# Relative attention and routed FFN on one core: the four weight tiles of a step turned in one stretch, the relative values in the bank of the value products

## The chip, the cores and the metric

The kernel is one program on one core of a Trainium2 chip. The metric is the device time of one execution in microseconds (us); lower is better. Timed runs of the same kernel are reported by their median. A profiled execution gives a trace with the start and duration of every instruction on every engine: PE is the matrix engine (TensorE; PEld are its weight loads), DVE the vector engine, ACT the scalar engine, POOL the general engine, SP the queue that issues most DMAs.

## The reference

The input is `x` of shape (16, 512, 128): 16 batches of 512 positions with 128 features. Everything is float32.

```python
q, k, v = proj(Wq, bq), proj(Wk, bk), proj(Wv, bv)      # 16 heads of 8 features, x normalized first
idx = clip(r[None, :] - r[:, None], -M, M) + M          # M = 128: relative place, cut at +-128
rpk, rpv = rel_k[idx], rel_v[idx]                        # (S, S, 8)
scores = (einsum('bhqd,bhkd->bhqk', q, k) + einsum('bhqd,qkd->bhqk', q, rpk)) / sqrt(8)
w = softmax(scores)
out = einsum('bhqk,bhkd->bhqd', w, v) + einsum('bhqk,qkd->bhqd', w, rpv)
x = x + layernorm(out @ Wo.T + bo)
# then: layernorm, top-1 routing to 16 experts, gated expert FFN and a shared FFN, layernorm, added to x
```

The second product of `out` needs, for each query, the weights of the keys that lie within 128 places of it times the relative values `rel_v`. Keys farther off all take the first or the last row of `rel_v`; the kernel adds those rows to `v` instead.

## The kernel before

**Two stages.** The attention stage computes all 16 batches and writes routed rows to DRAM; the FFN stage then reads blocks of 128 rows of one expert each. The change is in the attention stage alone.

**Steps.** The attention stage is one loop over steps `i`, 16 to a batch. `at(i)` gives batch `b`, unit `c` (one of 4) and `n` (one of 4); below, *step k* is the place `i % 16` in a batch, so `n` is `k % 4`. A step treats 32 queries and all 16 heads as four tiles of 128 x 512 scores, one for each head group `g` in the order `ORDER = (0, 2, 1, 3)`. They are called the first, second, third and fourth tile. All engines' instructions of this stage are kept in program order (the class `InOrder`, which is line 47 of every record), so the order of the lines of the loop is the order in each engine's queue.

**What a step does before the change.** In the order of the program:

- `scores` (PE): the content products (`ps<-kT,qb`, 32-row tiles of the array) and then the relative ones (`ps<-relk,qr`, 64-row tiles) into four PSUM banks of the pool `ps_s`. The relative ones go over a window of keys, 160 to 288 wide, which depends on the step; it is 288 wide in half of the steps.
- `turn` of the first and second tile of the step before (PE): four 128 x 128 transposes each (`pt<-ident,w`) into a bank of the pool `ps_t`, which has two.
- `peak` (DVE) and `exps` (ACT) of the first and second tile: the row maximum `nmax` and the exponentials `w` with their row sums. A score bank is free again when its `exps` is done.
- the copies of the two turned tiles out of PSUM to `wT`: the first by DVE, the second by ACT.
- `peak` and `exps` of the third and fourth tile.
- `attend` of the step five back (PE): the products of `wT` with the values (`pa<-wT,v`, 32-column tiles), into the first 128 columns of a bank of the pool `ps_o`, which has one; where `n == 1` also `join_places` (`pa<-oz,msum`) into the next 128 columns. Its `leave` runs at once: DVE copies out the join (`oj`), multiplies `pa` by the reciprocal sums and the head mask `Rh` (`od`) and adds the heads up (`oT`).
- `attend_near` of the same step (PE): the products with the relative values (`pz<-wT,relv`, 24 of them). They gather over the four steps of a unit in a bank of their own, `ps_z`; after the fourth DVE multiplies the whole bank by `Rz` in two instructions of 256 columns into `oz`.
- `turn` of the third tile and its copy by DVE.
- a spare job where there is one (`prt` in steps with `n == 0`, the output product `py` with `n == 1`, work for the next batch in steps 6, 7, 14 and 15), all in the one bank of `ps_o`.
- `turn` of the fourth tile and its copy by ACT. It needs the bank of the second tile.
- statistics and the routing of the batch before (`route`), a slice per step with `n > 0`: mostly small DVE work, and in a few steps a product in the bank of `ps_o` (`pr` in step 1, `ptf` in step 11, `pl` in step 13).

PE reads the transposed tiles four steps later, so the turn itself is not urgent. Four score banks, two of `ps_t`, one of `ps_o` and one of `ps_z` make up the eight banks of PSUM.

Of the kernel before, what the change touches and what calls it, by code (L numbers as in the profile page):

```python
# [9 lines left out]
F32 = mybir.dt.float32  # L10
# [4 lines left out]
PSUM = bass.MemoryType.PSUM  # L15
DRAM = bass.MemoryType.DRAM

P = 128
# [6 lines left out]
NKT = S // P  # L25
HG = 4
HH = H // HG
TQ = 8
# [22 lines left out]
def relative_attention_then_moe(  # L51
# [42 lines left out]
    with ExitStack() as actx:  # L94
# [3 lines left out]
        up = actx.enter_context(tc.tile_pool(name="attn_unit", bufs=2))  # L98
        sp = actx.enter_context(tc.tile_pool(name="attn_small", bufs=4))
        ps_s = actx.enter_context(tc.tile_pool(name="ps_s", bufs=4, space=PSUM))  # L100
        ps_t = actx.enter_context(tc.tile_pool(name="ps_t", bufs=2, space=PSUM))
        ps_o = actx.enter_context(tc.tile_pool(name="ps_o", bufs=1, space=PSUM))
        ps_z = actx.enter_context(tc.tile_pool(name="ps_z", bufs=1, space=PSUM))
        pe, act, dve, sp_q, pool = (InOrder(tc, e) for e in (nc.tensor, nc.scalar, nc.vector, nc.sync, nc.gpsimd))


# [323 lines left out]
        def join_places(pj, b, c):  # L430

            oz = batch.pop((b, c, "oz"))
            for h in range(HH):
                pe.matmul(
                    pj[h * 32 : (h + 1) * 32, :], msum.rearrange("p g d -> p (g d)"),
                    oz[:, h].rearrange("p t f q -> p (t f q)"), start=True, stop=True,
                )
            oj = up.tile([P, P], F32, tag="oj", name=f"oj{b}_{c}")
            batch[b, c, "oj"] = oj
            return lambda: dve.tensor_copy(oj, pj)  # L440

        def attend(b, c, n, done=None):


            wT = wts[b, c][0]
            v = batch[b]["v"]
            Rh = batch[b, c, "R"][0]
            if n == 0:
                batch[b, c, "oT"] = up.tile([P, NKT * 4, TQ], F32, tag="oT", name=f"oT{b}_{c}")
            oT = batch[b, c, "oT"]  # L450
            both = bank([P, 2, P], f"pa{b}_{c}_{n}")
            pa = both[:, 0]
            for kt in range(NKT):
                vn = 1 if kt <= n - 2 else 2 if kt >= n + 2 else 0
                for g in range(HG):
                    r = slice(g * 32, (g + 1) * 32)
                    pe.matmul(
                        pa[r, :], v[:, vn, kt, r], wT[:, n, g, (kt - n) % NKT, :],
                        start=(kt == 0), stop=(kt == NKT - 1),
                    )  # L460
            t = slice(n * 4, n * 4 + 4)
            summed = join_places(both[:, 1], *done) if done is not None else lambda: None

            def leave():
                summed()
                od = up.tile([P, 4, HH, TQ], F32, tag="od", name=f"od{b}_{c}_{n}")
                dve.tensor_mul(od, pa.rearrange("p (t h q) -> p t h q", h=HH, q=TQ), Rh[:, t])
                dve.tensor_reduce(oT[:, t], od.rearrange("p t h q -> p t q h"), AX.X, ALU.add)

            return leave  # L470

        def attend_near(b, c, n):


            wT = wts[b, c][0]
            if n == 0:
                batch[b, c, "pz"] = ps_z.tile([P, NKT, 8, HH, 4], F32, tag="z", name=f"pz{b}_{c}")
            pz = batch[b, c, "pz"]
            for u in (2 * n, 2 * n + 1):
                for k, n0, n1 in ((0, 0, 4), (3, 1, 4), (1, 0, 3)):  # L480
                    a = (P if k == 1 else -P if k == 3 else 0) - c * 32 - u * 4 + 252
                    for g in range(HG):
                        r = slice(g * 32, (g + 1) * 32)
                        pe.matmul(
                            pz[r, n0:n1, u],
                            relv[:, a : a + 4, :].rearrange("p t d -> p (t d)"),
                            wT[:, n0:n1, g, k, :].rearrange("p n (t h f q) -> p n t h f q", t=4, h=HH, f=2)[
                                :, :, u // 2, :, u % 2, :
                            ],
                            start=(k == 0), stop=(k == 1),  # L490
                        )
            if n < NKT - 1:
                return lambda: None
            wts.pop((b, c))
            Rz = batch.pop((b, c, "R"))[1]
            oz = up.tile([P, HH, NKT * 4, 2, 4], F32, tag="oz", name=f"oz{b}_{c}")
            batch[b, c, "oz"] = oz

            def leave():
                for f in range(2):  # L500
                    dve.tensor_mul(
                        oz[:, :, :, f, :].rearrange("p h t q -> p t h q"),
                        pz.rearrange("p n (t f) h q -> p (n t) f h q", f=2)[:, :, f],
                        Rz[:, :, :, f, :],
                    )

            return leave

# [217 lines left out]
        for i in range(total + 24):  # L726
            b, c, n = at(i)
            k = i % 16
            last = i - 1 if 0 <= i - 1 < total else None
            old = i - 5 if 0 <= i - 5 < total else None  # L730
            live = i < total
            done = at(i - 9)[:2] if n == 1 and 0 <= i - 9 < total else None
            nxt = b + 1 if b + 1 < B else None

            spare = None
            if 0 < b < B and k == 6:
                routes[b - 1, 0] = route(b - 1)

            if i == total + 1:
                routes[b - 1, 0] = route(b - 1, 0, NC - 1)  # L740
            if i == total + 5:
                routes[b - 1, 1] = route(b - 1, NC - 1, NC)
            if n == 0 and 0 <= i - 4 < total:
                sums(*at(i - 4)[:2])
                spare = lambda: sums_turn(*at(i - 4)[:2])
            if n == 1 and i >= 9 and i - 9 < total:
                spare = lambda: output(*at(i - 9)[:2])
            if 10 <= i < 30:
                clear_rows((i - 10) * NBLK // 20, (i - 9) * NBLK // 20)
            if nxt is not None:  # L750
                if k == 0 and b + 2 < B:
                    load_x(b + 2)
                if k in (6, 7, 14, 15):
                    f = {6: x_turn, 7: queries, 14: keys, 15: values}[k]
                    spare = lambda: f(nxt)

            if live:
                scores(b, c, n)
            if last is not None:
                T = {g: turn(*at(last), g) for g in ORDER[:2]}  # L760
            if live:
                peak(b, c, n, ORDER[0])
                peak(b, c, n, ORDER[1])
                exps(b, c, n, ORDER[0])
                exps(b, c, n, ORDER[1])
            if last is not None:
                dve.tensor_copy(*T[ORDER[0]])
                act.copy(*T[ORDER[1]])
            if live:
                peak(b, c, n, ORDER[2])  # L770
                peak(b, c, n, ORDER[3])
                exps(b, c, n, ORDER[2])
                exps(b, c, n, ORDER[3])
            if old is None and done is not None:
                join_places(bank([P, P], f"pj{b}"), *done)()
            if old is not None:
                attend(*at(old), done=done)()
                scale = attend_near(*at(old))
            if last is not None:
                dve.tensor_copy(*turn(*at(last), ORDER[2]))  # L780
            if old is not None:
                scale()
            if spare is not None:
                leave = spare()
            if last is not None:
                act.copy(*turn(*at(last), ORDER[3]))
            if spare is not None:
                leave()
            if nxt is not None and k in (0, 2):
                x_stats(nxt, k)  # L790
                x_stats(nxt, k + 1)
                if k == 2:
                    x_norm(nxt)

            for r in sorted(routes):


                turns = (n > 0) if nxt is not None else {7: 2, 9: 0, 12: 0, 13: 2, 15: 2}.get(k, 1) if live else 1
                for _ in range(turns):
                    bank_user = next(routes[r], StopIteration)  # L800
                    if bank_user is StopIteration:
                        del routes[r]
                        break
                    elif bank_user is not None:
                        bank_user()()
            if n == 1 and i + 3 < total:
                expand(*at(i + 3)[:2])
# [163 lines left out]
```

## Time and profile before

| | |
|---|---|
| median of 3 runs | 1973.37 us (1972.97 to 1974.53) |
| profiled execution | 1977.44 us, its span 1975.7 us |
| mean granted TensorE clock | 0.989 |
| PE busy | 1905.7 us (96%), 41070 matmuls |
| PEld busy | 1518.6 us (77%) |
| DVE busy | 1539.5 us (78%), 3922 instructions |
| ACT busy | 1154.3 us (58%) |
| POOL busy | 901.3 us (46%) |
| score matmuls (`ps`), first and last start | 23.0 and 1689.8 us |

Busy shares are averages over both stages. Matmuls overlap, so the time that a group of them holds PE is read from the starts of one group and the next, not from durations.

### The profile page before, as it was taken

The numbers are of one execution on the slowest core, as the hardware profiler recorded it, in microseconds if no ns is written. First come the engines' busy times: TensorE is split into PE (matmuls) and PEld (weight loads), VectorE is DVE, ScalarE is ACT, GpSimd is POOL, SyncE is SP. The second block draws the span as 40 slices with busy tenths as digits, with TensorE's granted clock in tenths as the row PEclk, the third lists the DMA queues.
The fourth block names the chain that finished last, engine by engine and source line by source line (L and its number), as shares of the span: only waits on it lengthen the run. The fifth ranks groups of instructions, "written<-read, shape, count | busy, mean of one in ns | idle before, by whom it ended". The sixth has DMA issues, their size and how long they took to land.

```text
span 1975.7 us, 92844 instructions
## 1 busy us (share of the span) xinstructions
PE 1905.7 (96%) x41070; PEld 1518.6 (77%) x41070; DVE 1539.5 (78%) x3922; ACT 1154.3 (58%) x2929; POOL 901.3 (46%) x1007
## 2 busy tenths in 40 slices
PE   6999999999999999999999999999999999689997
PEld 3777777777777777777777777777777777589997
DVE  4677787888787878787878888787878787757776
ACT  3666566666656666666666666666666666234432
POOL 4234454444444453535453544444444534246666
PEclk9999999999999999999999999999999999889999
DMA  2312000000000000000000000000000000066553
GB/s 75 69 30 42 14 23 5 14 14 6 22 5 24 5 23 3 25 3 25 3 25 3 25 3 16 12 12 16 5 18 5 18 7 5 13 176 176 173 165 95
DMA packets 88342, 68.94 MB, mean 35 GB/s; under 512 B 26439, under 2 KB 74340, under 8 KB 87808
## 3 DMA queue, kind: packets, MB, share of 16 engines
q1 hardware_dynamic: 81248, 53.60, 10.5%
q0 software_dynamic: 4384, 8.57, 1.2%
q8 instruction: 323, 5.29, 1.1%
q10 hardware_dynamic: 2304, 0.80, 0.2%
q14 instruction: 83, 0.68, 0.1%
HBM read 44.79 MB, written 18.75 MB: 32 GB/s over the span
## 4 chain that ended last, share of the span: by engine, by line
PE 80%; POOL 8%; DVE 6%; issue 5%; ACT 1%; DMA 1%; POOLq 0%; ACTq 0%; DVEq 0%; SPq 0%
PE ps L47 27%; PE pt L47 24%; PE pa L47 13%; PE pz L47 7%; POOL out_dram L912 4%; DVE nmax L47 3%; POOL lf_rs L80 2%; PE prt L47 2%; PE py L47 2%; POOL f L910 2%; PE pq L47 1%; PE pl L47 1%; PE pv L47 1%; PE pk L47 1%; DVE wT L47 1%
## 5 line engine op out<-in xcount | busy, mean ns | idle before, releaser
L47 ACT ACTIVATE w<-ps,nmax 128x512 f32<-128x512 f32 x1024 | 699.3, 693 | 497.7 <-DVE nmax L47 497.7
L47 DVE TENSOR_REDUCE nmax<-ps 128x1 f32<-128x512 f32 x1024 | 656.2, 683 | 288.3 <-PE ps L47 288.3
L47 PE MATMUL pt<-ident,w 128*128 128x128 f32 x4096 | 590.8, 280 | 3.1 <-DVE wT L47 2.7
L47 PEld LDWEIGHTS pt<-ident,w 128*128 128x128 f32 x4096 | 446.5, 141 | 139.0 <-issue 98.7
L47 ACT COPY wT<-pt 128x512 f32<-128x512 f32 x512 | 299.9, 586 | 129.0 <-PE pt L47 129.0
L47 DVE COPY wT<-pt 128x512 f32<-128x512 f32 x512 | 349.3, 682 | 1.6 <-PE pt L47 1.5
L47 PE MATMUL ps<-kT,qb 32*128 32x288 f32 (+10 forms) x4864 | 327.1, 375 | 5.4 <-POOL qb L47 3.8
L47 PE MATMUL pa<-wT,v 128*32 128x128 f32 x8192 | 276.7, 276 | 2.0 <-ACT R L47 1.2
L47 PE MATMUL ps<-relk,qr 64*32 64x288 f32 (+4 forms) x8192 | 275.2, 377 | 0.0
L47 PEld LDWEIGHTS ps<-kT,qb 32*128 32x128 f32 x4864 | 208.9, 186 | 62.9 <-issue 35.3
L47 PEld LDWEIGHTS pa<-wT,v 128*32 128x32 f32 x8192 | 208.0, 109 | 44.3 <-issue 41.6
L47 POOL TENSOR_TENSOR Rh<-R,mh 128x512 f32<-128x512 f32 x64 | 66.5, 1039 | 357.7 <-ACT R L47 351.2
L47 ACT ACTIVATION_READ_ACCUMULATOR w<-ps,nmax 128x1 f32 x1024 | 212.5, 208 | 0.0
L47 PEld LDWEIGHTS ps<-relk,qr 64*32 64x32 f32 x8192 | 124.4, 106 | 112.8 <-issue 82.8
L47 PE MATMUL pz<-wT,relv 128*32 128x48 f32 (+1 forms) x12288 | 192.1, 210 | 1.3 <-issue 1.3
L47 PEld LDWEIGHTS pz<-wT,relv 128*32 128x32 f32 x12288 | 184.1, 110 | 1.9 <-issue 1.9
L47 POOL TENSOR_TENSOR qr<-qz,mq 128x1024 f32<-128x1024 f32 x64 | 137.7, 2152 | 0.0
L47 POOL TENSOR_SCALAR kT<-kT,kend 128x512 f32<-128x512 f32 x32 | 49.8, 1562 | 145.0 <-ACT sg L47 128.3
L47 DVE TENSOR_REDUCE oT<-od 128x32 f32<-128x128 f32 x256 | 97.6, 381 | 8.9
L875 ACT ACTIVATE x2b<-x2b,xc 128x128 f32<-128x128 f32 x73 | 29.0, 401 | 125.2 <-DVE lf_ve L78 114.0
L47 POOL COPY rb<-rt 128x512 f32<-128x512 f32 x64 | 39.0, 609 | 116.6 <-DVE rt L47 104.7
L47 POOL DMA_INDIRECT rows<-pay,at_i x64 | 68.0, 1062 | 51.9 <-DVE shift L47 41.4
(157 smaller groups left out, 2241.8 us busy)
## 6 DMA issues: line engine op xcount, KB each, us to landing
gu<-_L_ffn_gate_up_proj_dram SPq DMA_DIRECT2D x73, 256.0 KB
dn<-in_L_ffn_down_proj_dram SPq DMA_DIRECT2D x73, 128.0 KB
rows<-zero SPq DMA_DIRECT2D x19, 266.0 KB
xc<-rows SPq DMA_DIRECT2D x8, 532.0 KB
x_sb<-in_L_attn_x_dram SPq DMA_DIRECT2D x64, 64.0 KB
qd<-qp SPq DMA_DIRECT2D x16, 256.0 KB
qz<-qd SPq DMA_DIRECT2D x248, 16.0 KB
relv<-vext SPq DMA_DIRECT2D x1, 1536.0 KB
```

Of the source, the lines that this page charges most:

```text
L47: return lambda *a, **k: self.tc.keep_in_program_order(op(*a, **k))
L80: root.tensor_tensor(rs, ve, mhalf[:, 0:n], ALU.pow)
L875: nc.scalar.mul(x2[:, 1, :], x2[:, 0, :], x[:, D + 2 : D + 3])
L910: nc.gpsimd.tensor_add(f, f, x[:, 0:D])
L912: own_rows("out", nc.gpsimd.indirect_dma_start(out_rows, bass.IndirectOffsetOnAxis(ap=to, axis=0), f, None, bounds_check=B * S - 1, oob_is ...
```

## The change

The pool `ps_t` gets a third bank and `ps_z` goes; PSUM stays at eight banks. A step is now `scores`, all four `peak` and `exps`, then on PE the values, the join and the near products, and then all four turns in one stretch, and after them the spare job. DVE copies the first tile after its four `peak`, ACT the second after its four `exps`; the fourth tile is turned into the bank of the first. The near products no longer gather over a unit: they go into columns 256 to 383 of the bank of the values, in the order (n, h, f, q), in runs of 4 columns instead of 16, and each step multiplies its own 128 columns by `Rz` into `oz`. The bank of `ps_o` is released after `od`, that product and, with `n == 1`, the copy `oj`.

```diff
-        ps_t = actx.enter_context(tc.tile_pool(name="ps_t", bufs=2, space=PSUM))
+        ps_t = actx.enter_context(tc.tile_pool(name="ps_t", bufs=3, space=PSUM))
         ps_o = actx.enter_context(tc.tile_pool(name="ps_o", bufs=1, space=PSUM))
-        ps_z = actx.enter_context(tc.tile_pool(name="ps_z", bufs=1, space=PSUM))
...
-            both = bank([P, 2, P], f"pa{b}_{c}_{n}")
-            pa = both[:, 0]
+            every3 = bank([P, 3, P], f"pa{b}_{c}_{n}")
+            pa = every3[:, 0]
...
+            near_done = attend_near(every3[:, 2], b, c, n)
 
             def leave():
-                summed()
                 od = up.tile([P, 4, HH, TQ], F32, tag="od", name=f"od{b}_{c}_{n}")
                 dve.tensor_mul(od, pa.rearrange("p (t h q) -> p t h q", h=HH, q=TQ), Rh[:, t])
+                near_done()
+                summed()
                 dve.tensor_reduce(oT[:, t], od.rearrange("p t h q -> p t q h"), AX.X, ALU.add)
...
-        def attend_near(b, c, n):
+        def attend_near(pn, b, c, n):
...
-                batch[b, c, "pz"] = ps_z.tile([P, NKT, 8, HH, 4], F32, tag="z", name=f"pz{b}_{c}")
-            pz = batch[b, c, "pz"]
-            for u in (2 * n, 2 * n + 1):
+                batch[b, c, "oz"] = up.tile([P, HH, NKT, 4, TQ], F32, tag="oz", name=f"oz{b}_{c}")
+            oz = batch[b, c, "oz"]
+            pz = pn.rearrange("p (n h f q) -> p n h f q", n=NKT, h=HH, f=2)
+            for f in range(2):
...
-                            pz[r, n0:n1, u],
+                            pz[r, n0:n1, :, f, :],
...
             def leave():
-                for f in range(2):
-                    dve.tensor_mul(
-                        oz[:, :, :, f, :].rearrange("p h t q -> p t h q"),
-                        pz.rearrange("p n (t f) h q -> p (n t) f h q", f=2)[:, :, f],
-                        Rz[:, :, :, f, :],
-                    )
+                dve.tensor_mul(
+                    oz[:, :, :, n, :].rearrange("p h n q -> p n h q"),
+                    pn.rearrange("p (n h q) -> p n h q", n=NKT, h=HH),
+                    Rz.rearrange("p (n t) h f q -> p n t h (f q)", t=4)[:, :, n],
+                )
...
             if live:
                 scores(b, c, n)
+                for g in ORDER:
+                    peak(b, c, n, g)
+                    exps(b, c, n, g)
+            if old is not None:
+                evicted = attend(*at(old), done=done)
+            elif done is not None:
+                evicted = join_places(bank([P, P], f"pj{b}"), *done)
             if last is not None:
-                T = {g: turn(*at(last), g) for g in ORDER[:2]}
-            if live:
-                peak(b, c, n, ORDER[0])
-                peak(b, c, n, ORDER[1])
-                exps(b, c, n, ORDER[0])
-                exps(b, c, n, ORDER[1])
-            if last is not None:
+                T = {g: turn(*at(last), g) for g in ORDER[:3]}
                 dve.tensor_copy(*T[ORDER[0]])
                 act.copy(*T[ORDER[1]])
-            if live:
-                peak(b, c, n, ORDER[2])
-                peak(b, c, n, ORDER[3])
-                exps(b, c, n, ORDER[2])
-                exps(b, c, n, ORDER[3])
-            if old is None and done is not None:
-                join_places(bank([P, P], f"pj{b}"), *done)()
-            if old is not None:
-                attend(*at(old), done=done)()
-                scale = attend_near(*at(old))
-            if last is not None:
-                dve.tensor_copy(*turn(*at(last), ORDER[2]))
-            if old is not None:
-                scale()
+                T[ORDER[3]] = turn(*at(last), ORDER[3])
+            if old is not None or done is not None:
+                evicted()
             if spare is not None:
                 leave = spare()
             if last is not None:
-                act.copy(*turn(*at(last), ORDER[3]))
+                dve.tensor_copy(*T[ORDER[2]])
+                act.copy(*T[ORDER[3]])
             if spare is not None:
                 leave()
```

More of the change, by code (lines that the diff above doesn't have):

```diff
@@ L435, in join_places @@
                     pj[h * 32 : (h + 1) * 32, :], msum.rearrange("p g d -> p (g d)"),
-                    oz[:, h].rearrange("p t f q -> p (t f q)"), start=True, stop=True,
+                    oz[:, h].rearrange("p n t q -> p (n t q)"), start=True, stop=True,
                 )
@@ L461, in attend @@
             t = slice(n * 4, n * 4 + 4)
-            summed = join_places(both[:, 1], *done) if done is not None else lambda: None
+            summed = join_places(every3[:, 1], *done) if done is not None else lambda: None
+            near_done = attend_near(every3[:, 2], b, c, n)
             def leave():
-                summed()
                 od = up.tile([P, 4, HH, TQ], F32, tag="od", name=f"od{b}_{c}_{n}")
                 dve.tensor_mul(od, pa.rearrange("p (t h q) -> p t h q", h=HH, q=TQ), Rh[:, t])
+                near_done()
+                summed()
                 dve.tensor_reduce(oT[:, t], od.rearrange("p t h q -> p t q h"), AX.X, ALU.add)
             return leave
-        def attend_near(b, c, n):
+        def attend_near(pn, b, c, n):
             wT = wts[b, c][0]
             if n == 0:
-                batch[b, c, "pz"] = ps_z.tile([P, NKT, 8, HH, 4], F32, tag="z", name=f"pz{b}_{c}")
-            pz = batch[b, c, "pz"]
-            for u in (2 * n, 2 * n + 1):
+                batch[b, c, "oz"] = up.tile([P, HH, NKT, 4, TQ], F32, tag="oz", name=f"oz{b}_{c}")
+            oz = batch[b, c, "oz"]
+            pz = pn.rearrange("p (n h f q) -> p n h f q", n=NKT, h=HH, f=2)
+            for f in range(2):
                 for k, n0, n1 in ((0, 0, 4), (3, 1, 4), (1, 0, 3)):
-                    a = (P if k == 1 else -P if k == 3 else 0) - c * 32 - u * 4 + 252
+                    a = (P if k == 1 else -P if k == 3 else 0) - c * 32 - (2 * n + f) * 4 + 252
                     for g in range(HG):
@@ L484, in attend_near @@
                         pe.matmul(
-                            pz[r, n0:n1, u],
+                            pz[r, n0:n1, :, f, :],
                             relv[:, a : a + 4, :].rearrange("p t d -> p (t d)"),
                             wT[:, n0:n1, g, k, :].rearrange("p n (t h f q) -> p n t h f q", t=4, h=HH, f=2)[
-                                :, :, u // 2, :, u % 2, :
+                                :, :, n, :, f, :
                             ],
@@ L491, in attend_near @@
                         )
[L492 to L497, printed above, removed]
-            def leave():
-                for f in range(2):
-                    dve.tensor_mul(
-                        oz[:, :, :, f, :].rearrange("p h t q -> p t h q"),
-                        pz.rearrange("p n (t f) h q -> p (n t) f h q", f=2)[:, :, f],
-                        Rz[:, :, :, f, :],
-                    )
+            Rz = batch[b, c, "R"][1]
+            if n == NKT - 1:
+                wts.pop((b, c))
+                batch.pop((b, c, "R"))
+            def leave():
+                dve.tensor_mul(
[3 more added lines that the diff above has]
+                )
             return leave
```

## The prediction

> **What bounds the kernel now.** I read the page first, part 1 and part 4, then the waits, then one ordinary step in the timeline, engine by engine, and last the records of single instructions for the distances from start to start.
>
> ```profile
> PE 1905.7 (96%) x41070; PEld 1518.6 (77%) x41070; DVE 1539.5 (78%) x3922; ACT 1154.3 (58%) x2929; POOL 901.3 (46%) x1007
> PE ps L47 27%; PE pt L47 24%; PE pa L47 13%; PE pz L47 7%; POOL out_dram L912 4%; DVE nmax L47 3%; POOL lf_rs L80 2%; PE prt L47 2%; PE py L47 2%; POOL f L910 2%; PE pq L47 1%; PE pl L47 1%; PE pv L47 1%; PE pk L47 1%; DVE wT L47 1%
> ```
>
> The chain that ended last lies on PE for four fifths, in the groups of the attention step. The waits say that PE there waits for almost nobody: the entries with a releaser are small, those marked issue are the changes between groups.
>
> ```profile
> DVE nmax L47 <- PE ps L47: 288.3, 227, 6.1
> PEld ps L47 <- ACT w L47: 8.6, 21, 1.7
> PE prt L47 <- DVE od L47: 7.6, 14, 0.5
> PEld pt L47 <- DVE wT L47: 3.9, 5, 0.9
> ```
>
> DVE waits for the scores in 227 steps of 256, so it is not the bound, but 1.3 us a time is all the slack it has. Step 10 of a batch, PE and then DVE (start, duration, instruction):
>
> ```profile
> 819.56 1.20 PE L47 MATMUL ps<-relk,qr 64*32 64x288 f32 x32
> 820.69 1.09 PE L47 MATMUL pt<-ident,w 128*128 128x128 f32 x8
> 821.72 1.08 PE L47 MATMUL pa<-wT,v 128*32 128x128 f32 x32
> 822.61 0.75 PE L47 MATMUL pz<-wT,relv 128*32 128x64 f32 x48
> 823.29 1.09 PE L47 MATMUL pt<-ident,w 128*128 128x128 f32 x8
> ...
> 820.43 1.29 DVE L47 TENSOR_REDUCE nmax<-ps 128x1 f32<-128x512 f32 x2 [0.74 <-PE ps L47]
> 821.64 0.68 DVE L47 COPY wT<-pt 128x512 f32<-128x512 f32 x1
> 822.24 1.28 DVE L47 TENSOR_REDUCE nmax<-ps 128x1 f32<-128x512 f32 x2
> 823.43 0.28 DVE L47 TENSOR_TENSOR od<-pa,Rh 128x128 f32<-128x128 f32 x1
> 823.75 0.38 DVE L47 TENSOR_REDUCE oT<-od 128x32 f32<-128x128 f32 x1
> 824.05 0.68 DVE L47 COPY wT<-pt 128x512 f32<-128x512 f32 x1
> ```
>
> The next scores begin at 824.31. The copy of the first tile ends at 822.32 and its bank is wanted at 823.29: there is 1 us of room. That room is what the change spends.
>
> **What PE saves.** Inside a stretch, transposes start 0.109 us apart. Where the shape of the array's tiles changes, the distance from the last start of one group to the first of the next is longer: relative scores to turn 0.333 (0.197 would be the pace, so 0.137 more), turn to values 0.203 (0.094 more), near products to turn 0.137 (0.115 more). The first transpose of a stretch then takes 0.165 to the second (0.056 more). The change has one stretch of turns instead of two, so a turn-to-values change and one change into turns go. What comes is a change straight from relative scores to values, which no row shows. Its bounds are 0.094 over the pace (turn to values) and 0.137 (relative scores to turn). I take 0.116: the 0.094, and the 0.022 that relative scores cost more than near products before the same turns. So 0.203 + 0.137 + 0.056 - 0.109 - 0.116, about 0.17 us less in a step; 0.149 to 0.192 by the bounds.
>
> **What the fourth tile's bank takes back.** The fourth tile goes into the bank of the first, and DVE now copies that only after four reductions. Step 10 again, rebuilt: values begin at 819.56 + 0.798 (last relative start) + 0.312 = 820.67, near products 0.897 later at 821.57, the first turn 0.678 later at 822.25. Its last transpose starts 0.383 later and takes 0.273; DVE starts 0.037 after that (the distance in the rows where DVE waited for a turn) at 822.94. DVE itself is free at 820.43 plus four reductions of 0.60 to 0.61, 822.85, so the turn decides here. The copy ends 0.683 later, PE's weight load follows 0.053 after a DVE release: 823.68. Without the wait the fourth tile's load would have been due at 823.50. After a load that waited, the second transpose follows 0.167 later (as at `prt` now), so PE loses 0.12 us in this step. The next scores begin at 823.68 + 0.167 + 0.218 + 0.202 = 824.27, 0.05 earlier than now. **Of 0.17 us, 0.12 is handed back.** With a relative window narrower than 288 the reductions decide instead of the turn, by up to 0.16 us more.
>
> **The sixteen steps of a batch**, each worked like this against its measured length:
>
> - Steps 2, 6, 8, 10, 12, 14: -0.05, -0.10, -0.20, -0.05, -0.14, -0.06. More than 0.05 where the spare job now stands waiting for `od` to give up its bank (0.07 to 0.17 in the `prt` steps); behind the fourth tile that bank is free in time, 1.13 us after the first copy starts against 1.23. Steps 7, 11, 15 (narrower windows): -0.13, -0.12, -0.13; step 11 loses its 0.15 wait for the last exponential, since ACT no longer copies a tile (0.465 us) between the second and third. Together -0.98.
> - Steps 5 and 9: the output product needs `oj`, now third in DVE's row after `od` and the near product (0.2 us each): +0.10 each.
> - Steps 1 and 13: `pr` and `pl` need the bank of the output product, which DVE empties (`y_sb`) after copying the third tile: 2.15 us after the first copy begins, 0.5 later in the step than now: +0.53 each.
> - Steps 0, 3 and 4. DVE is late here already, by the routing work and x statistics queued ahead of its reductions:
>
> ```profile
> 775.14 0.18 DVE L47 TENSOR_TENSOR ahead<-upto,nb 128x16 f32<-128x16 f32 x1
> 775.35 0.17 DVE L47 SCALAR_TENSOR_TENSOR ahead<-ahead,shift 128x16 f32<-128x16 f32 x1
> 775.45 1.28 DVE L47 TENSOR_REDUCE nmax<-ps 128x1 f32<-128x512 f32 x2
> ...
> 778.75 1.86 PE L47 MATMUL ps<-kT,qb 32*128 32x320 f32 x16
> ```
>
> The reduction is that of step 3: it starts 2.57 after the scores (772.88), 0.6 later than it would in step 12's pattern with the same window. PE pays in step 4, where the content products take 1.8 us instead of 1.08, waiting for the exponentials. After the change DVE has 2.24 us of such work behind the third copy, its reduction comes 2.81 after the scores, and PE pays at once for the bank: 2.81 + 2.42 + 1.32 = 6.55 against 5.87, +0.68. Step 4 then finds its score banks free: -0.92. In step 0 the values' copy is behind the spare job `pv`, which moves to the end of step 15: +0.27. Together +0.03.
>
> Sum: -0.98 + 0.20 + 1.06 + 0.03 = +0.3 us a batch, +4.6 for 15 batches; the first has no routing and gains about 0.5. **+4 us.**
>
> **What else is added.** DVE's near product costs 256 x 0.28 (the row of `od`, same size) against 128 x 0.41 removed: 19 us of DVE, in the slack of 1.3 us a step except in steps 0 and 3, where it is counted. Two of the four reductions of a step now carry a separate wait instruction more; the reduction that has one today starts 0.608 instead of 0.598 after the last, 0.02 a step, counted. No DMA is moved; POOL's `Rz` ends at 814.93 in a unit whose first `od` starts at 816.84, so it is ready though it is now used three steps sooner. The near products write runs of 4 columns instead of 16; no row has such a run. Bounds: nothing (they already read runs of 4), or their 0.54 us doubled. I take nothing, since the reading side is the same pattern.
>
> The Trainium skill speaks against that last edit: "PSUM — Partial Sum Buffer", Specifications (TRN2), says that a non-contiguous pattern slows matmuls significantly, with lines of 8 bytes. If that held for runs of 16 bytes as well, an estimate by the same doubling would add 251 x 0.54 = 136 us; if it holds only below a line, nothing.
>
> **The rivals.**
>
> *The third bank hides the copy.* If the fourth tile doesn't wait, 251 steps keep 0.15 to 0.19 us: 37 to 48 us less, 1925 to 1936. For it: three banks, and PE waits only 3.9 us for such copies today. Against it: the start of the copy is bound twice over, by the turn itself and by four reductions. 15%.
>
> *DVE's lateness goes straight to PE* (slower). Place: DVE's queue between the third copy and the next reductions. It decides where that work exceeds about 1.3 us, as in steps 2, 15 and after 1 and 13. If step 4 gives back half or none of its 0.92 because DVE doesn't catch up, 7 or 14 us more, and if the upper bound of the new group change and a near product as dear as one of today's (0.41) cost 0.05 in every step, 13 on top: 1984 to 2004. 32%.
>
> *Short runs in PSUM.* The near products at twice their 0.54 us: 251 x 0.54 = 136, about 2113. Nothing in the trace for it. 5%.
>
> **How the numbers follow.** Forecast, 48%: what the turns save comes back as bank waits, +4 us. The sum is made against the profiled execution, 1977.4 us (span 1975.7 and 1.7 around it): 1981.4. The median of the runs lies 4.1 below it, 1973.4, so the forecast there is 1977. An error of 0.05 us a step, the width of the new group change, is 13 us, so the case reaches from 1960 to 1993. A measurement can tell about 0.2%, 4 us: faster means below 1969.4, slower above 1977.3. Of the forecast's 48, 15 fall faster, 18 the same, 15 slower; with the rivals faster 0.30, same 0.18, slower 0.52. The range 1952 to 2002 leaves out the hidden copy and the short runs.
>
> **What would show it.** Right: one run of 16 transposes a step; a wait of `pt` for DVE's `wT` copy of some 0.1 us in over 200 steps, no longer 5; values 0.29 to 0.33 after the last relative score at 288 wide; step 3 about 6.5 and step 4 about 6.0 us. Wrong: no such wait; near products longer than 0.54 from first to last start; DVE without idle time ahead of `nmax`.

## The result, and the profile after

| | before | after |
|---|---|---|
| median | 1975.17 us (1972.97 to 1978.67, 20 runs) | 1978.66 us (1975.32 to 1982.15, 20 runs) |
| ratio, 95% interval | | 1.0018 [1.0011, 1.0024] |
| profiled execution, span | 1977.44, 1975.7 us | 1979.73, 1978.0 us |

The changed kernel is slower by 3.5 us, less than 0.2%. The forecast of 1977 us lies 1.7 us below it. In the two profiled executions the spans differ by 2.3 us. But the difference does not come from where the prediction had it, as will be seen.

The page's busy times and its chain that ended last, of the changed kernel:

```profile
PE 1878.5 (95%) x41070; PEld 1504.8 (76%) x41070; DVE 1537.1 (78%) x4050; ACT 1146.3 (58%) x2929; POOL 903.5 (46%) x1007
PE ps L47 25%; PE pt L47 21%; PE pa L47 19%; DVE wT L47 4%; POOL out_dram L902 4%; DVE nmax L47 4%; POOL lf_rs L80 2%; POOL f L900 2%; PE prt L47 1%; PE py L47 1%; PE pl L47 1%; PE pq L47 1%; PE pk L47 1%; PE pv L47 1%; DVE pay L47 1%
```

PE is busy for 27 us less, and the span is no shorter. What is new in the chain is DVE with `wT` (4%, 1% before): the chain now goes from PE through DVE's copy and back in about half of the steps. The waits show the same (engine, line, releaser, then us in total, times, longest):

```profile
PEld pt L47 <- DVE wT L47: 40.7, 64, 1.7
PE pt L47 <- DVE wT L47: 26.7, 33, 1.4
PEld py L47 <- DVE oj L47: 11.4, 63, 0.7
```

`pt` behind `wT` was 3.9 us. The view leaves the shortest waits out: in the single records from 100 to 1640 us the fourth tile's first weight load comes 0.053 to 0.055 us after the end of DVE's copy 234 times, in practically every step. Step 10 of a batch, PE and then DVE (start, duration, instruction):

```profile
929.51 0.75 PE L47 MATMUL pa<-wT,relv 128*32 128x64 f32 x48
930.19 2.10 PE L47 MATMUL pt<-ident,w 128*128 128x128 f32 x16
932.22 0.55 PE L47 MATMUL ps<-kT,qb 32*128 32x320 f32 x4
...
928.36 2.48 DVE L47 TENSOR_REDUCE nmax<-ps 128x1 f32<-128x512 f32 x4 [0.39 <-PE ps L47]
930.88 0.69 DVE L47 COPY wT<-pt 128x512 f32<-128x512 f32 x1
```

One run of 16 transposes, 2.10 us long where 16 at 0.109 with a first distance of 0.165 would be done in 1.97: the first copy ends at 931.57, the fourth tile waits for it. The step takes 5.978 us, before 5.998.

**Where the 3.5 us are.** From the first scores of one batch to those of the next, the middle batches take 104.61 us before and 104.66 after, the last (up to the scores of its last step) 98.2 and 96.5, and the first 103.4 and 107.3. In the middle batches the change costs next to nothing; the loss is in the first batch. There PE stands still in the middle of groups, for nothing that the profile shows ("issue"):

```profile
92.41 1.14 PE L47 MATMUL pt<-ident,w 128*128 128x128 f32 x9 [1.68 <-issue]
97.23 0.30 PE L47 MATMUL pa<-wT,relv 128*32 128x48 f32 x9 [0.31 <-issue]
106.19 0.51 PE L47 MATMUL pa<-wT,relv 128*32 128x48 f32 x25 [3.25 <-issue]
```

These are matmuls number 1241, 1369 and 1497 of the program: 128 apart, with their weight loads 256 instructions. Before, the stops are at 1242, 1370 and 1498 and take 0.19, 0.30 and 0.19 us. In this stretch the DMA view shows the zeroing of the row buffer, nearly all pieces of 266 KB, fourteen of the twenty issued within 16 us, and PE's instructions arriving through the same engines (queue, packets, MB, share of the 16 engines, from 84 to 108 us):

```profile
q1 hardware_dynamic: 7289, 3.72, 99.4%
q8 instruction: 4, 0.07, 1.2%
```

The Trainium skill, "Runtime: NRT & Kernel Launch", Instruction fetch mechanics, says that an engine's instructions come in blocks of 256 through a DMA queue of its own, and calls the crossing of a block mostly hidden. The trace agrees with the 256: the stops are so far apart, and the 323 packets of q8 in the whole run would be 82688 instructions, for PE's 82140 matmuls and weight loads. Hidden the crossing is not while the queues are full.

**Two stretches at half clock.** In the profile's rows the granted TensorE clock is 1.00 in almost all of the steps, but each of the two profiles has one stretch of 3.41 us at 0.50: the changed kernel in step 12 of the first batch, 1.4 us after the third stop, and the kernel before in step 1 of the last batch (window, length, busy time of PE, PEld, DVE, ACT and POOL, granted clock, DMA share, GB/s; the changed kernel first):

```profile
107.58:110.99 3.41, 3.41 (x26) 3.08 (x28) 1.74 (x5) 1.76 (x3) 0.00 (x0) 0.50 0.00 0
1598.20:1601.61 3.41, 3.41 (x35) 2.00 (x42) 1.02 (x8) 0.00 (x0) 3.41 (x4) 0.50 0.00 0
```

Each cost about 1.4 us: the step of the kernel before takes 7.95 us there, and 6.56 in its run with the zeroing spread (below), where the clock stays at 1.00. So the last batch's 98.2 against 96.5 us is hardly a gain of the change: without such a stretch the kernel before takes 96.6. Why the clock fell there is not shown.

### The profile page after: what moved, and what is told of

Read it like the earlier page. It is cut to its first block, busy times and chain, and to the rows that moved or that the text cites. A ratio compares the mean times of both kernels' runs of the same rounds, so it can differ in the third digit from the quotient of the medians.

```text
span 1978.0 us, 93290 instructions
## 1 busy us (share of the span) xinstructions
PE 1878.5 (95%) x41070; PEld 1504.8 (76%) x41070; DVE 1537.1 (78%) x4050; ACT 1146.3 (58%) x2929; POOL 903.5 (46%) x1007
## 4 chain that ended last, share of the span: by engine, by line
PE 71%; DVE 13%; POOL 8%; issue 5%; DMA 1%; ACT 0%; SPq 0%; POOLq 0%; DVEq 0%; ACTq 0%
PE ps L47 25%; PE pt L47 21%; PE pa L47 19%; DVE wT L47 4%; POOL out_dram L902 4%; DVE nmax L47 4%; POOL lf_rs L80 2%; POOL f L900 2%; PE prt L47 1%; PE py L47 1%; PE pl L47 1%; PE pq L47 1%; PE pk L47 1%; PE pv L47 1%; DVE pay L47 1%
## 5 line engine op out<-in xcount | busy, mean ns | idle before, releaser
L47 ACT ACTIVATE w<-ps,nmax 128x512 f32<-128x512 f32 x1024 | 690.7, 687 | 605.6 <-DVE nmax L47 605.4
L47 DVE TENSOR_REDUCE nmax<-ps 128x1 f32<-128x512 f32 x1024 | 634.4, 682 | 271.0 <-PE ps L47 271.0
L47 PE MATMUL pt<-ident,w 128*128 128x128 f32 x4096 | 543.0, 280 | 28.3 <-DVE wT L47 26.7
L47 PEld LDWEIGHTS pt<-ident,w 128*128 128x128 f32 x4096 | 439.8, 141 | 89.1 <-DVE wT L47 40.7
L47 PE MATMUL ps<-kT,qb 32*128 32x288 f32 (+10 forms) x4864 | 308.9, 374 | 4.9 <-POOL qb L47 3.8
L47 ACT COPY wT<-pt 128x512 f32<-128x512 f32 x512 | 288.7, 598 | 20.9 <-PE pt L47 20.3
L47 PEld LDWEIGHTS ps<-kT,qb 32*128 32x128 f32 x4864 | 195.1, 186 | 74.2 <-ACT wT L47 21.8
L47 ACT ACTIVATION_READ_ACCUMULATOR w<-ps,nmax 128x1 f32 x1024 | 207.4, 203 | 0.0
L47 PE MATMUL pa<-wT,relv 128*32 128x48 f32 (+1 forms) x12288 | 192.3, 210 | 4.2 <-issue 4.2
L47 PEld LDWEIGHTS pa<-wT,relv 128*32 128x32 f32 x12288 | 184.3, 110 | 4.7 <-issue 4.7
```

Of the source, the lines that this page charges most:

```text
L47: return lambda *a, **k: self.tc.keep_in_program_order(op(*a, **k))
```

## The experiments

The kernel before ran beside each of them: 1976.82 us (17 runs) beside the score bank, the bank with the order, the near products alone and the moved work; 1975.36 (15 runs) beside the order alone, the stretch alone, the changed kernel with the zeroing spread and the first of the faster versions; 1975.65 (15 runs) beside the kernel before with the zeroing spread and the last version. Ratios are to it.

### A bank more for the first tile

The theory of the prediction is that PE pays for the bank that the fourth tile waits for. So the changed kernel with the first tile turned into a score bank, which leaves the three of `ps_t` to the others:

```diff
-            pt = ps_t.tile([P, NKT, P], F32, tag="t", name=f"pt{b}_{c}_{n}_{g}")
+            if g == ORDER[0]:
+                pt = ps_s.tile([P, S], F32, tag="s", name=f"pt{b}_{c}_{n}_{g}").rearrange("p (k j) -> p k j", k=NKT)
+            else:
+                pt = ps_t.tile([P, NKT, P], F32, tag="t", name=f"pt{b}_{c}_{n}_{g}")
```

> The changed kernel, with one thing more: the first tile of a step is turned into the score bank that the first tile's exponentials have just released, so the second, third and fourth tiles have the three turn banks for themselves and the fourth never waits for the first one's copy. Theory A (several limits at the same place): the wait of the fourth tile goes, but behind it stands the spare job, whose bank DVE releases 1.13 us after the copy of the first tile starts, so that only steps without a spare job gain: steps 2, 3 and 10 of a batch by 0.12 to 0.15 us each, 0.4 us a batch, 6 us below the changed kernel (about 1972, ratio to the kernel before about 0.998 to 1.000). Rival B (the bank wait alone eats the gain of the turns): 0.12 to 0.26 us in each of 251 steps, 30 to 45 us below the changed kernel, ratio 0.98.

Measured: 1979.93 us, ratio 1.0016 [1.0008, 1.0025]. No gain at all: theory B's 30 to 45 us are out, and the small gain of theory A did not come either. And yet the wait is gone. Step 8 of the changed kernel and then of this one, PE and DVE:

```profile
916.94 2.10 PE L47 MATMUL pt<-ident,w 128*128 128x128 f32 x16
918.88 0.62 PE L47 MATMUL prt<-ident,rb 128*128 128x128 f32 x4
...
918.44 0.28 DVE L47 TENSOR_TENSOR oz<-pa,Rz 128x128 f32<-128x128 f32 x1
```

```profile
917.50 1.97 PE L47 MATMUL pt<-ident,w 128*128 128x128 f32 x16
919.43 0.63 PE L47 MATMUL prt<-ident,rb 128*128 128x128 f32 x4
...
919.00 0.28 DVE L47 TENSOR_TENSOR oz<-pa,Rz 128x128 f32<-128x128 f32 x1
```

The stretch is 0.13 us shorter, and the spare job starts as late as before: 0.15 to 0.16 us after DVE has finished `oz` in both (918.88 less 918.72, 919.43 less 919.28). `prt` needs the bank of the values, and this bank is handed back by the same DVE queue, behind the same copy. Over all steps, from last transpose to `prt` 0.109 became 0.235 us, to `py` 0.208 became 0.432. Only the steps without a spare job keep their 0.13 (step 2: 5.876 to 5.746, step 10: 5.978 to 5.847). The steps with `py` are 0.06 to 0.07 us longer than in the changed kernel, and a batch 0.23. So two waits of nearly the same length lay one behind the other, and the prediction had given a price only to the first.

### The bank, and DVE empties the values first

```diff
             if last is not None:
                 T = {g: turn(*at(last), g) for g in ORDER[:3]}
+            added = evicted() if old is not None or done is not None else None
+            if last is not None:
                 dve.tensor_copy(*T[ORDER[0]])
                 act.copy(*T[ORDER[1]])
                 T[ORDER[3]] = turn(*at(last), ORDER[3])
-            if old is not None or done is not None:
-                evicted()
+            if added is not None:
+                added()
```

`evicted` now does `od`, `oz` and `oj`, and hands back the head sum `oT`, which is done behind the first copy.

> As the run with the score bank, and in addition DVE empties the value bank (od, near product, oj) before it copies the first tile; only the sum over heads stays behind that copy. Theory A: now neither the fourth tile nor the spare job waits, PE runs densely in all steps but 0 and 3, and each step is 0.12 to 0.27 us shorter than in the changed kernel: about 2.6 us a batch, 42 us in all, near 1936, ratio to the kernel before 0.980. Rival B: the order on DVE adds nothing to what the bank gives, so both runs are equal.

Measured: 1927.39 us, ratio 0.9751 [0.9738, 0.9764], more than was expected. Step 8 again:

```profile
890.41 1.97 PE L47 MATMUL pt<-ident,w 128*128 128x128 f32 x16
892.21 0.60 PE L47 MATMUL prt<-ident,rb 128*128 128x128 f32 x4
...
891.22 0.28 DVE L47 TENSOR_TENSOR oz<-pa,Rz 128x128 f32<-128x128 f32 x1
```

Now `oz` ends at 891.50, before the turn is over, and `prt` follows the last transpose at the pace, 0.109. `py` does too. All steps are shorter than in the changed kernel: 0 by 0.22, 1, 5 and 13 by 0.33, 9 by 0.26, the others by 0.05 to 0.27, 3.1 us in a batch.

### The order alone

The same diff on the changed kernel, without the score bank.

> The changed kernel, with one edit: DVE empties the bank of the values (od, the near product, the join where there is one) before it copies the first turned tile; the head sum stays behind. No further bank for the tile.
> Theory A (both banks are handed back by DVE one behind the other, so one waits longer when the other goes first): the first copy starts 0.4 us later (two instructions of 0.20 each), 0.6 with n == 1, so the fourth tile waits 0.5 us instead of 0.13; the spare jobs lose their wait of at most 0.1. Some 0.4 us a step, 251 steps: about 2070 us, ratio 1.045 to 1.058 to the kernel before.
> Theory B (only the bank of the values is late, the fourth tile's wait is no limit, and the gain of 49 us came from the order alone): 1925 to 1940 us, ratio 0.975 to 0.983.

Measured: 2054.6 us, ratio 1.0404 [1.0388, 1.042]. So theory A holds, though the loss is a little less than it said. The wait:

```profile
PEld pt L47 <- DVE wT L47: 113.3, 187, 1.7
```

The fourth tile's bank comes 0.26 us later (step 10: 6.240 against 5.978) and not 0.4, since `od` follows the reductions at once, 2.40 us after the first began, so that the copy starts at 2.80, while it had to wait for the turn until 2.52 when it went first. Each edit alone brings nothing or does harm, 1.0016 and 1.0404; both together 0.9751.

### One stretch without the third bank

The stretch alone: near products in `ps_z` as before, two banks of `ps_t`. The lines of the turns, against the changed kernel:

```diff
-        ps_t = actx.enter_context(tc.tile_pool(name="ps_t", bufs=3, space=PSUM))
+        ps_t = actx.enter_context(tc.tile_pool(name="ps_t", bufs=2, space=PSUM))
...
-                T = {g: turn(*at(last), g) for g in ORDER[:3]}
+                T = {g: turn(*at(last), g) for g in ORDER[:2]}
                 dve.tensor_copy(*T[ORDER[0]])
                 act.copy(*T[ORDER[1]])
+                T[ORDER[2]] = turn(*at(last), ORDER[2])
                 T[ORDER[3]] = turn(*at(last), ORDER[3])
```

> One part of the change alone: all four tiles turned in one stretch after the values, but the near products in the bank of their own as before, and so two banks for the tiles instead of three.
> Theory A (a stretch needs a bank for each tile that DVE or ACT can't copy in time): the third tile waits for the first copy, some 0.5 us, and the fourth for ACT's copy, which comes after four exponentials, so that a step like step 10 takes 6.8 us instead of 6.0: some 0.8 us a step, 170 to 210 us more, ratio 1.085 to 1.105.
> Theory B (the stretch saves its 0.15 us a step and the copies keep up): 1935 to 1950 us, ratio 0.98 to 0.987.

Measured: 2150.11 us, ratio 1.0884 [1.0867, 1.09]; step 10 takes 6.75 us. The third tile waits for DVE's copy, the fourth for ACT's:

```profile
PEld pt L47 <- DVE wT L47: 171.0, 255, 2.1
PEld pt L47 <- ACT wT L47: 86.4, 199, 0.7
```

### The near products alone

The other half: before's turns and two banks, but the near products in the bank of the values.

```diff
-                attend(*at(old), done=done)()
-                scale = attend_near(*at(old))
+                attend(*at(old), done=done)()
             if last is not None:
                 dve.tensor_copy(*turn(*at(last), ORDER[2]))
-            if old is not None:
-                scale()
```

(`attend` and `attend_near` are those of the changed kernel.)

> The kernel before with one part of the change alone: the near products in the bank of the value products, multiplied step by step; the order of the turns and the two turn banks as before, the bank of ps_z unused. Theory A: DVE releases the value bank one product (0.20 us) later, and the spare jobs stand right behind it: steps 0, 4, 6, 7, 8, 12, 14, 15 lose 0.2 us each and pr and pl in steps 1 and 13 the same; 1.6 to 2.0 us a batch, 25 to 31 us above the kernel before, ratio about 1.014. Rival D: this part is free, since DVE has 1.3 us of slack a step, ratio 1.000.

Measured: 2040.31 us, ratio 1.0325 [1.0312, 1.0338], more than twice what was expected. The products themselves cost nothing more, 0.541 us from first to last start. The price is the bank. Step 5, PE and DVE:

```profile
925.84 0.66 PE L47 MATMUL pt<-ident,w 128*128 128x128 f32 x4
926.88 0.46 PE L47 MATMUL py<-wo,oT 128*128 128x128 f32 x2 [0.38 <-DVE oj L47]
...
926.04 0.29 DVE L47 TENSOR_TENSOR od<-pa,Rh 128x128 f32<-128x128 f32 x1 [0.27 <-PE pa L47]
926.45 0.28 DVE L47 COPY oj<-pa 128x128 f32<-128x128 f32 x1
```

DVE can begin to empty the bank only when the near products are done, and three instructions (`od`, `oz`, `oj`) stand between; `py` starts 0.656 us after the last transpose instead of 0.109. Steps with a spare job grow by 0.2 us (`prt`), 0.47 to 0.56 (`py`) or 0.26 (the projections), those without by 0.05 at most: 4.0 us in a batch. In the changed kernel the 16 transposes between values and spare job cover most of this. So neither half of the change stands alone, 1.0884 and 1.0325; together they come out even.

### Work moved out of DVE's way

In steps 0 and 3 of the changed kernel DVE is late. So the changed kernel, with the second pair of x statistics (and the normalization behind it) moved from step 2 to step 4 and the projection to values from step 15 to 10:

```diff
-                if k in (6, 7, 14, 15):
-                    f = {6: x_turn, 7: queries, 14: keys, 15: values}[k]
+                if k in (6, 7, 10, 14):
+                    f = {6: x_turn, 7: queries, 10: values, 14: keys}[k]
...
-            if nxt is not None and k in (0, 2):
+            if nxt is not None and k in (0, 4):
```

> The changed kernel with DVE's work in other steps: the second pair of x statistics (and the normalization behind it) moves from step 2 to step 4, the values of the next batch from step 15 to step 10. Nothing is left out. Theory A (a late DVE reaches PE through the first tile's copy at once): step 3 falls from 6.50 to about 5.85 us, step 0 from 6.77 to about 6.5; steps 10 and 15 exchange about 0.9 us; in sum 0.9 us a batch, 14 us below the changed kernel, ratio to the kernel before about 0.995. Rival C (these steps are bound by POOL or by the exponentials): steps 3 and 0 stay as they are, ratio 1.002.

Measured: 2018.87 us, ratio 1.0217 [1.0203, 1.023]: a miss. The reason for the move was right: step 3 falls from 6.504 to 5.700 us and step 0 from 6.774 to 5.852, so DVE's queue was what made them long. The work comes back elsewhere: step 15 less 0.9 and step 10 plus 0.9 (the projection itself), step 6 plus 1.8, step 11 plus 2.1. In seven batches one step more (step 12, once step 7) is 1.6 us longer; each time the granted clock is 0.50 there for 3.41 us, so that some 11 of the 42 us are the clock's and not the queues'. Why it fell so often is not shown. In step 6 small DVE instructions take as long as whole tiles, with POOL's `qr`, which now comes behind the normalization, beside them:

```profile
915.33 1.77 DVE L47 CAST at_i<-at_f 128x4 int32<-128x4 f32 x1
...
914.92 2.15 POOL L47 TENSOR_TENSOR qr<-qz,mq 128x1024 f32<-128x1024 f32 x1
```

The cast takes 0.17 us in the changed kernel (at most 0.171 in 17) and 1.76 here in the median; it ends at 917.10, POOL's instruction at 917.07. All 13 casts that took so long end 0.02 to 0.03 us after that instruction. In step 11 the four `ptf` wait for POOL's `x`, which is behind the two additions to `v` there. That both moves did harm is read from the steps' lengths; they were not run one by one.

### The zeroing spread

The stops of the first batch, put to the test: each zeroing DMA reads a tile that POOL clears in its step, so that SP issues about one a step.

```diff
         def clear_rows(n0, n1):
+            nought = sp.tile([P, PW], F32, tag="nought", name=f"nought{n0}")
+            pool.memset(nought, 0.0)
             sp_q.dma_start(
                 rows.rearrange("(n p) w -> p n w", p=P)[:, n0:n1, :],
-                zero.unsqueeze(1).to_broadcast([P, n1 - n0, PW]),
+                nought.unsqueeze(1).to_broadcast([P, n1 - n0, PW]),
             )
```

> The changed kernel, with the zeroing of the row buffer spread: each of its 20 DMAs takes a small tile that POOL sets to zero in that step, so that SP issues them one a step instead of all at 82 to 99 us.
> Theory A (the first batch's stops of PE, 1.68, 0.31 and 3.25 us, each 128 matmuls after the last, are late blocks of instructions behind the zeroing): none of them over 0.3 us, batch 0 down from 107.3 to about 103 us, about 4 to 5 us less: ratio 0.9990 to 1.0000 to the kernel before.
> Theory B (the stops belong to the code and not to the zeroing): they stay at the same matmuls, ratio 1.0018 as without the edit.

Measured: 1972.27 us, ratio 0.9987 [0.9978, 0.9996]. The DMA view from 84 to 108 us has the zeroing at a seventh of what it was, and no stop of PE over 0.15 us is left at these matmuls; batch 0 takes 99.3 us, 8.0 less and so less than was expected: the three stops had cost 5.8 from start to start, the half clock behind them 1.5, and step 1 is 0.8 shorter, in which the full clock comes at 33.8 us instead of 35.9.

```profile
q1 hardware_dynamic: 1984, 1.02, 14.6%
```

The kernel before with the same edit:

> The kernel before, with the zeroing of the row buffer spread as in the changed kernel's run (a small tile set to zero by POOL in each of 20 steps).
> Theory A (late blocks of instructions cost the kernel before only 0.19 to 0.30 us a stop in its profile, but up to a few us in other executions): faster by 0.5 to 3 us, ratio 0.9985 to 0.9998. The changed kernel with the same edit is then within 0.1% of it, as the middle batches of the two, 104.61 and 104.66 us, say.
> Theory B (the zeroing disturbs only the changed kernel): no difference, ratio 1.0000; the changed kernel with the edit stays 0.13% ahead.

Measured: 1974.08 us, ratio 0.9990 [0.9981, 0.9999]. Without the crowd of the first batch the two kernels can't be told apart, 0.9987 and 0.9990. The 0.18% by which the changed one was slower shows only where the zeroing comes all at once, and not in the steps that the change remade. Why the changed kernel's blocks came later than those of the kernel before stays open: in one profile its stops sum to 5.2 us, in the kernels with the score bank, the order or the moved work to between 1.8 and 3.6.

### The faster version

The kernel of 0.9751, and in steps 1 and 13 the output product ahead of the fourth tile and `y_sb` ahead of DVE's copy of the third:

```diff
-                T[ORDER[3]] = turn(*at(last), ORDER[3])
+                if k not in (1, 13):
+                    T[ORDER[3]] = turn(*at(last), ORDER[3])
...
             if spare is not None:
                 leave = spare()
+                if k in (1, 13):
+                    leave()
             if last is not None:
+                if k in (1, 13):
+                    T[ORDER[3]] = turn(*at(last), ORDER[3])
                 dve.tensor_copy(*T[ORDER[2]])
                 act.copy(*T[ORDER[3]])
-            if spare is not None:
+            if spare is not None and k not in (1, 13):
                 leave()
```

> The kernel with the score bank and the emptied bank of the values, with one edit in steps 1 and 13: the output product goes ahead of the fourth tile, and DVE's y_sb ahead of the copy of the third tile.
> Theory A (in these steps PE stands 0.66 us behind the output product, because no turn is left to cover the latency of y_sb; the row: 0.743 from the last output product to the router's product with four transposes between them in the kernel before, against 0.659 without): 0.66 + 0.44 - 0.74, some 0.35 us less in each, 30 steps, 10 us less than without the edit: 1915 to 1920 us, ratio 0.969 to 0.972.
> Theory B (DVE's queue is late there in any case): no difference, ratio 0.975.

Measured: 1916.48 us, ratio 0.9706 [0.9693, 0.9719]. Steps 1 and 13 are each 0.437 us shorter, four transposes' pace: the whole fourth tile fits into the latency of `y_sb`. In step 1:

```profile
840.22 0.39 PE L47 MATMUL py<-wo_h,oj 128*128 128x128 f32 x2
840.44 0.60 PE L47 MATMUL pt<-ident,w 128*128 128x128 f32 x4
840.99 0.43 PE L47 MATMUL pr<-oh,before 128*128 128x64 f32 x2
```

The edit of the zeroing added to it:

> The score bank for the first tile, the bank of the values emptied first, the fourth tile behind the output product in steps 1 and 13, and the zeroing spread: all that helped in one kernel.
> Theory A (the first batch's stops add to the rest): 2 to 5 us less than without the spread zeroing, 1911 to 1915 us, ratio 0.968 to 0.9695.
> Theory B (the stops' cover is used up, or POOL's 20 memsets come back in the first steps): 1916 us, ratio 0.9706.

Measured: 1913.16 us, ratio 0.9682 [0.9669, 0.9695], 3.2% faster than the kernel before. No stop is left in its first batch.

## Why the prediction was right, and where it was not

**What PE saves: 0.17 us, in truth 0.15.** The term that was off is the one for the new change of groups, relative scores to values. It was taken at 0.116 us over the pace between bounds of 0.094 and 0.137; it measured 0.333 from start to start, exactly what relative scores to turn took, so 0.136. The upper bound was right.

**What the bank takes back: 0.12 us.** Right: step 10 is 0.131 us longer with the wait than with the score bank, and 0.02 shorter than before, where 0.05 was said.

**The sixteen steps.** Predicted and measured difference per step, us:

| step | 0 | 1 | 2 | 3 | 4 | 5 | 6 | 7 | 8 | 9 | 10 | 11 | 12 | 13 | 14 | 15 |
|---|---|---|---|---|---|---|---|---|---|---|---|---|---|---|---|---|
| predicted | .27 | .53 | -.05 | .68 | -.92 | .10 | -.10 | -.13 | -.20 | .10 | -.05 | -.12 | -.14 | .53 | -.06 | -.13 |
| measured | .20 | .47 | -.02 | .63 | -.92 | .12 | -.07 | -.21 | -.15 | .12 | -.02 | -.13 | -.09 | .47 | -.11 | -.24 |

The sum is +0.05 us a batch instead of +0.3; no step is off by more than 0.11, and every sign is right. The work on the queues, instruction by instruction, holds. Step 3 is 6.504 us (about 6.5 was said), step 4 5.945 (about 6.0).

**The first batch** is the step that failed: it was to gain about 0.5 us and lost 3.9, in stops for instructions that no row of before shows at that size (0.30), and in the half clock behind them. The right total is luck, made of two errors that meet. To the last scores the span grew by 1.7 us: +3.9 in the first batch instead of -0.5, and -2.1 in the other fifteen instead of +4.6 (the rest, 0.6, is the FFN stage); 1.4 of the 2.1 is the half clock in the last batch of before. The two profiles with the zeroing spread, which have neither the stops nor a half clock behind step 1, show more of what belongs to the change: the first batch takes 102.6 us before and 99.3 after, the other fifteen together 1559.4 and 1559.2. So the change by itself gains some 3 us in the first batch, more than the 0.5 that was said, and next to nothing in the others, where +4.6 was said. By these profiles its own part of the total is nearer -3 than +4, too little for the timed runs to tell (0.9990 and 0.9987).

**Near products.** `oz` costs 0.28 us a step as taken from `od`; the runs of 4 columns in PSUM are free, 0.541 us from first to last start in the kernel before, in the changed one and in the run with them alone. The sentence of "PSUM — Partial Sum Buffer", Specifications (TRN2), that any non-contiguous pattern slows matmuls does not hold for runs of 16 bytes here; the rival that stood on it is out. Nor are the runs dearer than contiguous columns: four value products of 128 contiguous columns go out every 0.109 us, four near products of 64 columns every 0.056.

**The rivals.** The third bank doesn't hide the copy: 234 fourth tiles waited. DVE's lateness goes to PE in step 3, and step 4 gives it back in full, 0.92.

**What the prediction didn't see** is that the wait it named was not alone. It put a price on the values' bank only in the steps with `oj` and `y_sb`; elsewhere it found this bank free in time by 0.1 us (1.13 against 1.23), which holds only as long as the fourth tile waits. With the first wait taken away the bank of the values holds PE up by the same amount, and moving near products into it costs 64 us by itself, as the experiment showed. The forecast survived because one limit covered the other.

## What to carry to other kernels

When an engine hands back two banks from one queue, ask of both when they are needed: taking one wait away shows nothing while the other stands right behind it, and the order of the queue and the number of banks have to be changed together. Fewer changes of an array's tile shape are worth their 0.09 to 0.14 us each only where the longer stretch has a bank for each tile. And compare kernels batch by batch, with the granted clock beside each stretch, before an explanation of a difference of 0.2% is begun: here it lay in the first of sixteen, in a crowd of transfers that the change does not touch and in a stretch at half clock.

## What the runs showed of the hardware

- PE's instructions can be late. With the 16 DMA engines full of zeroing (99.4% on one queue), PE stood 1.68, 0.31 and 3.25 us at matmuls 128 apart, 256 instructions with the weight loads; with the zeroing spread no stop over 0.15 us was left there.
- A small DVE instruction beside a POOL instruction can last until that one ends: the cast to integers 1.76 us instead of 0.17, `lx_ve` 0.91 instead of 0.17, the product `place` 0.81 instead of 0.19. The Trainium skill, "SBUF — State Buffer", Who interferes with whom, says that the two engines share a pair of ports which one of them can hold for a whole instruction while the other is blocked; the ends, 917.10 and 917.07 us, agree.
- A change from relative scores (64-row tiles) to products of 32-column tiles costs as much as one to full transposes, 0.136 us over the pace.
- The granted clock can fall to 0.50 for 3.41 us in the midst of busy steps: once in this stage of each of the two profiles (at 107.58 and 1598.20 us), eight times in the run with the moved work. It made a step some 1.4 to 1.6 us longer. What brings it on is not shown.
